# The output products of an attention block: 32 channels of o stacked under c2, the other 64 as half pieces

## The chip, the cores and the metric

The kernel runs on one core of a Trainium2 chip. The metric is the device time of one execution in microseconds: the median of 3 runs is 6416.27 us, the lowest 6413.48, the highest 6428.01. The profile is of one further execution.

## The reference

The input is x, four images of 96 channels and 128 x 128 pixels, all in f32. A state-space block (convolution, scans in four directions, normalisation over channels, a projection from 192 to 96 channels) comes first, and its result is normalised in groups. The second block takes that result, here called xnew, and computes:

```python
xr, x1, x2 = _relu_split_norm(x, sc1, sc2, res_coef, nc1, nc2)
y1 = NORM_SCALE * _layer_norm(_attn_conv(x1, x2, aw1, aw2, aw3))
y2 = NORM_SCALE * _layer_norm(_conv2d(x2, w_conv2, K // 2)) * x1
y = jnp.concatenate([y1, y2], axis=1)
return xr + _conv2d(y, w_full, 0) + b_full[None, :, None, None]
```

So for every pixel the output has a part that is linear in the value of xnew on each side of a threshold (the residual and xr), plus a matrix of 96 x 192 times the 192 values of y. 96 of those come from the attention convolution (o in the kernel) and 96 from an ordinary convolution (c2), normalised and multiplied by x1. The layer norms are over a whole image, so the last product can begin only when o and c2 of the image are complete and their means and variances known. The normalisation is folded into the weights and a bias.

## The kernel before

The images go one after the other. For an image b there is first a norm (`ssm_output`: the scan's result is normalised, projected and added to the input, giving xnew), a split (`split_norm`), the attention convolution (`attention`, products at L1477 and L1492, their results copied by ScalarE and combined by VectorE in `outputs`, L1550 to L1573) and last the close (`attn_output`), which makes the output of the image. Python generators emit the instructions: `co_run` emits the convolution of image b (the left side) and, between its steps, pieces of lighter work (the right side): norm and split of image b+1, then the close of image b-1. What remains of the right side is emitted before the next convolution begins. Each `yield` names an estimated cost in microseconds by which the two are dealt out.

For the first phase, up to the end of the scan, `in_order` (L339) ties every instruction to the one before it on its engine. After L2561 nothing does: the framework's planner orders the instructions of each engine by their place in the program and by when it expects them to be ready. The result is seen in the trace: the program emits the o product and the c2 product of one half, then of the other, and the trace has both halves' o products first and then both halves' c2 products. Each engine then runs its own list in order, and a wait holds what is behind it. Loads and stores go through SP's queue, also in order.

The close of images 0, 1 and 2 is `attn_output`, L2299 to L2341. The last image has its own form (`LastOutput`), which shares `own_weights`, `c2_weights`, `first_half` and `residual` with it. In `attn_output`:

- `own_weights` (L2259) forms mean and variance of o, scales the first 96 x 96 part of the weights by the inverse deviation into w1, and writes the bias as row 96 of w1 by two products of one row and a copy. `c2_weights` (L2224) does the same for c2, giving w2; its mean is in s2.
- The bias row is met by a row of ones: `with_ones` makes tiles of 97 partitions whose last row is set by GpSimd (L2278) once, and o is loaded into the first 96.
- An image is cut into NS = 16 tiles of SN = 1024 pixels, and each tile into two halves of CH = 512 pixels[...] (`part`, from the pool `psr`, which has two banks). Loads of the next tile are issued ahead: o (L2312), c2 and xx, which is xnew (L2315), 384 KB each, from DRAM.
- For a tile, ScalarE computes x1 (L2283), VectorE masks it (L2284), VectorE makes c2 = (c2 - mean) * x1 in place (L2326). `residual` makes e: ScalarE the upper line (L2288), VectorE the mask (L2289) and then e = xx * low + e (L2290).
- For each half, TensorE makes the product of w1 and o (97 rows, L2334) and, in the same bank, of w2 and c2 (96 rows, L2335). VectorE adds e and writes the result over x1 (L2337 for image 0; L2339 with another order of the pixels for images 1 and 2). A store takes x1 to the output (L2341).

The norm contains a projection of 192 channels to 96 (L1023 and L1028) in which 128 channels are one product and the other 64 lie as two pieces, each half of the pixels on one half of the partitions.

Of the kernel before, what the change touches and what calls it, by code (L numbers as in the profile page):

```python
# [9 lines left out]
F32 = mybir.dt.float32  # L10
BF16 = mybir.dt.bfloat16
AF = mybir.ActivationFunctionType
ALU = mybir.AluOpType
# [4 lines left out]
C = 96  # L18
H = W = 128
L = H * W  # L20
CH = 512
# [32 lines left out]
SN = 1024  # L54
# [17 lines left out]
def kernel(  # L72
# [26 lines left out]
    nc = tc.nc  # L99
# [6 lines left out]
    def load(src, name):  # L106
        t = const.tile(list(src.shape), F32, name=name, tag=name)
        nc.sync.dma_start(t, src)
        return t
# [44 lines left out]
    def filled(value, name, n=C, p=C):  # L154
        t = const.tile([p, n], F32, name=name, tag=name)
        nc.vector.memset(t, value)
        return t

    mean96 = filled(1.0 / C, "mean96")
# [17 lines left out]
    def col(name, width=1, bufs=None):  # L177
        return small.tile([C, width], F32, name=name, tag=name, bufs=bufs)

    def rsqrt(dst, var):  # L180

        t = col("rsq")
        nc.vector.tensor_scalar(t, var, GN_EPS, None, ALU.add)
        nc.scalar.activation(t, t, AF.Sqrt)
        nc.vector.reciprocal(dst, t)

    def combine(ps, stats, mat, name, mv=None):


        if mv is None:  # L190
            mv = small.tile([stats.shape[0], 2], F32, name="mv", tag=f"mv{stats.shape[0]}")
            nc.vector.bn_aggr(mv, stats)  # L192
        n = mv.shape[0]
        p1 = bank(ps)[:n, 0:2]
        nc.tensor.matmul(p1, lhsT=mat, rhs=mv, start=True, stop=True)  # L195
        r = small.tile([n, 2], F32, name=name, tag=name)
        nc.vector.tensor_copy(r, p1)
        d2 = small.tile([n, 1], F32, name=f"d2{n}", tag=f"d2{n}")
        nc.vector.tensor_sub(d2, mv[:, 0:1], r[:, 0:1])
        nc.vector.tensor_mul(d2, d2, d2)  # L200
        p2 = bank(ps)[:n, 0:2]
        nc.tensor.matmul(p2[:, 0:1], lhsT=mat, rhs=d2, start=True, stop=True)  # L202
        nc.vector.tensor_add(r[:, 1:2], r[:, 1:2], p2[:, 0:1])
        return r, mv
# [84 lines left out]
    def bank(ps):  # L289

        return ps.tile([128, CH], F32, name="bank", tag="bank")

    def part(ps, *shape):
        n = 1
        for d in shape[1:]:
            n *= d
        t = bank(ps)[: shape[0], :n]
        return t if len(shape) == 2 else t.rearrange("p (a b) -> p a b", b=shape[2])
# [1922 lines left out]
            yield from lift(H)  # L2221
            later.flush()

    def c2_weights(img, ps, pool):  # L2224


        n = NSTRIP
        mva, mvb = (pool.tile([128, 2], F32, name=f"mv_{i}") for i in "ab")
        for mv, st, p, e, k in (
            (mva, img.c2a, 96, 128, 4 * n - img.mapped),  # L2230
            (mvb, img.c2b, 0, 64, 2 * n - (not img.mapped)),
            (mvb, img.c2b, 64, 128, 2 * n - 1),
        ):
            v = st[p:e, :k].rearrange("p c s -> p (c s)")
            nc.vector.bn_aggr(mv[p:e], v)
        halves = ((mva[96:128], m96[96:128]), (mvb, mrows[img.mapped]))

        def over(n):
            pt = bank(ps)[:, 0:n]
            for i, (mv, mat) in enumerate(halves):  # L2240
                nc.tensor.matmul(
                    pt, lhsT=mat, rhs=mv[:, 0:n], start=(i == 0), stop=(i == 1)
                )
            return pt

        s2 = pool.tile([128, 2], F32, name="s2")
        nc.vector.tensor_copy(s2, over(2))
        for mv, p in ((mva, 96), (mvb, 0)):
            d = mv[p:128, 0:1]
            nc.vector.tensor_sub(d, d, s2[p:128, 0:1])  # L2250
            nc.vector.tensor_mul(d, d, d)
        nc.vector.tensor_add(s2[:, 1:2], s2[:, 1:2], over(1))
        r2 = col("r2")
        rsqrt(r2, s2[0:C, 1:2])
        w2 = pool.tile([C, C], F32, name="w2")
        nc.vector.tensor_scalar(w2, wful[:, 1], r2, None, ALU.mult)
        return s2, w2

    def own_weights(img, ps, pool):  # L2259

        so, _ = combine(ps, img.ost.rearrange("p c s -> p (c s)"), mean96, "so")
        ro = col("ro")
        rsqrt(ro, so[:, 1:2])
        w1 = pool.tile([128, C], F32, name="w1")
        nc.vector.tensor_scalar(w1[0:C], wful[:, 0], ro, None, ALU.mult)
        nso = col("nso")
        nc.vector.tensor_scalar(nso, so[:, 0:1], -1.0, None, ALU.mult)
        pt = bank(ps)[C : C + 1, 0:C]  # L2270
        nc.tensor.matmul(pt, lhsT=img.keep["low"][:, 1:2], rhs=ident, start=True, stop=False)
        nc.tensor.matmul(pt, lhsT=nso, rhs=w1[0:C], start=False, stop=True)  # L2272
        nc.vector.tensor_copy(w1[C : C + 1], pt)
        return w1[0 : C + 1]

    def with_ones(pool, name, bufs=None):
        y = pool.tile([128, SN], F32, name=name, tag=name, bufs=bufs)
        nc.gpsimd.memset(y[C : C + 1], 1.0)  # L2278
        return y[0 : C + 1]

    def first_half(img, xx, x1):
        thr, scale, shift = (img.keep[n] for n in ("thr", "scale", "shift"))
        nc.scalar.activation(x1, xx, AF.Identity, scale=scale[:, 0:1], bias=shift[:, 0:1])  # L2283
        nc.vector.scalar_tensor_tensor(x1, xx, thr, x1, ALU.is_gt, ALU.mult)  # L2284

    def residual(img, xx, e):
        up, low, thr = (img.keep[n] for n in ("up", "low", "thr"))
        nc.scalar.activation(e, xx, AF.Identity, scale=up[:, 0:1], bias=up[:, 1:2])  # L2288
        nc.vector.scalar_tensor_tensor(e, xx, thr, e, ALU.is_gt, ALU.mult)  # L2289
        nc.vector.scalar_tensor_tensor(e, xx, low[:, 0:1], e, ALU.mult, ALU.add)  # L2290

    def pixels(v):

        return v.rearrange("p (h j t) -> p h t j", j=TW, t=TN)

    def plain(v):
        return v.rearrange("p (h t j) -> p h t j", j=TW, t=TN)

    def attn_output(img, ps, side, share):  # L2299
        ob = out[img.b].rearrange("c h w -> c (h w)")  # L2300
        with (
            tc.tile_pool(name="f1", bufs=1, side=side) as p1,
            tc.tile_pool(name="f3", bufs=2, side=side) as p3,
        ):
            w1 = own_weights(img, ps, p1)
            s2, w2 = c2_weights(img, ps, p1)
            ones = [with_ones(p1, f"o{i}") for i in range(2)]

            def loads(t):
                o = ones[t % 2]  # L2310
                got = [o]
                nc.sync.dma_start(o[0:C], img.od[:, bass.ts(t, SN)])  # L2312
                for name, src in (("c2", img.c2d), ("xx", img.xnew)):
                    y = p3.tile([C, SN], F32, name=name)
                    nc.sync.dma_start(y, src[:, bass.ts(t, SN)])  # L2315
                    got.append(y)
                return got

            ahead = loads(0)
            for t in range(NS):  # L2320
                o, c2, xx = ahead
                if t + 1 < NS:
                    ahead = loads(t + 1)
                x1 = p3.tile([C, SN], F32, name="x1")
                first_half(img, xx, x1)
                nc.vector.scalar_tensor_tensor(  # L2326
                    c2, c2, s2[0:C, 0:1], x1, ALU.subtract, ALU.mult
                )
                e = p3.tile([C, SN], F32, name="e")
                residual(img, xx, e)  # L2330
                for h in range(2):
                    sl = bass.ts(h, CH)
                    pf = part(ps, C, CH)
                    nc.tensor.matmul(pf, lhsT=w1, rhs=o[:, sl], start=True, stop=False)  # L2334
                    nc.tensor.matmul(pf, lhsT=w2, rhs=c2[:, sl], start=False, stop=True)  # L2335
                    if img.mapped:
                        nc.vector.tensor_add(x1[:, sl], pf, e[:, sl])  # L2337
                    else:
                        nc.vector.tensor_add(plain(x1[:, sl]), pixels(pf), pixels(e[:, sl]))  # L2339
                    yield 2.6 * share  # L2340
                nc.sync.dma_start(ob[:, bass.ts(t, SN)], x1)  # L2341

# [103 lines left out]
    class Image:  # L2446
# [44 lines left out]
        def close(self, ps, side, share=1.0):  # L2491
            while not self.finished:
                at.later.tick()
            yield from attn_output(self, ps, side, share)
# [27 lines left out]
    with tc.tile_pool(name="wp", bufs=1, side="left") as wp:  # L2522
# [7 lines left out]
        for images, pace in (([0], 0.25), ([1], 0.75), ([2, 3], 1.35)):  # L2530
            left = projections(images, weights, stats, wp, psl)
            if images[0] == 0:
# [12 lines left out]
                got = next(others)  # L2545
                while not got:
                    next(left)
                    got = next(others)
# [25 lines left out]
    wful = load(w_full, "wful")  # L2574
# [123 lines left out]
```

## Time and profile before

| what | value |
|---|---|
| median of 3 runs | 6416.27 us |
| profiled execution | 6409.68 us, span 6407.8 us |
| mean granted clock of TensorE | 0.902 |
| busy share of the span | TensorE 82%, VectorE 73%, ScalarE 59%, GpSimd 51% |
| close of image 0: first o product, last evacuation starts | 4646.0 us, 4777.2 us |
| close of image 1 and 2: evacuations (L2339) start | 5461.2 to 5905.8 us |
| o products, L2334 | 192 instructions, 105.5 us busy |
| c2 products, L2335 | 192 instructions, 108.2 us busy |
| DMA | 1205.30 MB, 188 GB/s mean |

An f32 product of one half shows as two matmul instructions, so a tile has four of L2334 and four of L2335. Busy time counts overlapping instructions once, while the mean duration of one is counted in full; the durations of matmuls overlap, and what a product costs TensorE is seen from one start to the next. In a group, the idle time is that of the engine just ahead of the group's instructions, with what ended it.

### The profile page before, as it was taken

Reading aid. Unit: us, or ns where it says so; the run is one execution under the profiler, and the core shown is the slowest. Engines: PE = TensorE matmul, PEld = TensorE weight load, DVE = VectorE, ACT = ScalarE, POOL = GpSimd, SP = SyncE. Lnnn points to the kernel's source line nnn. Section 1 sums busy time; section 2 is a strip of 40 time slices with the busy share of each in tenths; the row PEclk is TensorE's granted clock in tenths of the full one; section 3 lists DMA queues with packets and bytes.
Section 4 is the critical chain, followed back from the end, with each engine's and each line's share of the span. In section 5 each row is a group of like instructions: output and inputs, shape, how many; then the busy total and the mean of one; then the engine's idle time right before and its main releaser. Section 6 shows DMA issues by size and latency. Waiting matters only on the chain. (4 is left out here: it accounts for less than half of the span.)

```text
span 6407.8 us, 76468 instructions
## 1 busy us (share of the span) xinstructions
PE 5253.4 (82%) x23264; PEld 2254.8 (35%) x23264; DVE 4699.9 (73%) x7132; ACT 3759.4 (59%) x4770; POOL 3238.6 (51%) x2476
## 2 busy tenths in 40 slices
PE   6889988987888643989988588977888877889888
PEld 2333322322222111444433234345333444345553
DVE  4247878988989768989844686468774687988767
ACT  1247767787787666777622465466644665545642
POOL 1326757978879554979822234436304365022310
PEclk9899989998999765999999799989989888999989
DMA  6766777775675766676667686665776656967668
GB/s 155 175 160 189 198 199 199 214 221 163 198 202 171 202 183 207 196 213 179 182 185 195 166 228 163 195 169 156 214 199 184 175 149 165 245 167 180 191 168 221
DMA packets 897706, 1205.30 MB, mean 188 GB/s; under 512 B 230644, under 2 KB 745642, under 8 KB 884816
## 3 DMA queue, kind: packets, MB, share of 16 engines
q1 hardware_dynamic: 866640, 1145.36, 65.5%
q0 software_dynamic: 16336, 38.51, 2.3%
q10 hardware_dynamic: 14320, 16.54, 0.9%
q8 instruction: 187, 3.06, 0.2%
q14 instruction: 223, 1.83, 0.1%
HBM read 777.82 MB, written 345.62 MB: 175 GB/s over the span
## 5 line engine op out<-in xcount | busy, mean ns | idle before, releaser
L633 PE MATMUL bank<-y,wp 128*128 128x512 f32 (+3 forms) x3584 | 1310.9, 622 | 83.8 <-DMA y<-y 41.0
L866 POOL TENSOR_TENSOR y<-y,dl 128x1024 f32<-128x1024 f32 x384 | 1058.5, 2757 | 263.0 <-DVE dl L858 240.3
L833 POOL TENSOR_TENSOR dl<-dl,u 128x1024 f32<-128x1024 f32 x384 | 1008.8, 2627 | 253.1 <-ACT dA L809 121.1
L854 DVE TENSOR_TENSOR_SCAN dA<-dA,pBC 128x512 f32<-128x512 f32 x768 | 981.6, 1278 | 30.7
L2169 PE MATMUL bank<-y,wn 128*64 128x384 f32 (+5 forms) x2408 | 680.1, 507 | 58.3 <-DMA y<-x1d 34.1
L1477 PE MATMUL two<-ya,wd 128*64 128x192 f32 (+3 forms) x2376 | 582.2, 414 | 174.0 <-ACT odd L1550 65.1
L633 PEld LDWEIGHTS bank<-y,wp 128*128 128x128 f32 (+3 forms) x3584 | 456.2, 168 | 749.3 <-issue 651.1
L858 DVE TENSOR_TENSOR dl<-dA,pBC 128x512 f32<-128x512 f32 x768 | 528.5, 688 | 255.8 <-PE pBC L747 183.8
L747 PE MATMUL pBC<-xr,wbc 60*128 60x512 bf16 (+1 forms) x1536 | 457.8, 404 | 311.5 <-DVE dA L854 239.1
L1938 ACT COPY yb<-ya 64x768 f32<-64x768 f32 (+1 forms) x660 | 537.7, 815 | 195.5 <-PE two L1477 113.8
L676 ACT ACTIVATE dl<-pd,dtb 128x512 f32<-128x512 f32 x768 | 485.5, 684 | 187.9 <-PE pd L747 171.5
L1477 PE MATMUL two<-yb,wd 128*64 128x192 f32 (+3 forms) x2376 | 559.0, 400 | 4.0 <-ACT yb L1938 4.0
L837 DVE TENSOR_TENSOR pBC<-dl,pBC 128x512 f32<-128x512 f32 x768 | 527.5, 687 | 8.8 <-POOL dl L833 7.8
L2169 PEld LDWEIGHTS bank<-y,wn 128*64 128x64 f32 (+3 forms) x2408 | 310.3, 169 | 357.2 <-issue 186.2
L809 ACT ACTIVATE dA<-dl,negA 128x1024 f32<-128x1024 f32 x384 | 420.3, 1141 | 2.3
L1477 PEld LDWEIGHTS two<-ya,wd 128*64 128x64 f32 (+1 forms) x2376 | 262.2, 165 | 370.9 <-ACT odd L1550 75.0
L676 ACT ACT_TABLE_LOAD x248 | 318.2, 1283 | 91.9 <-PE pd L747 79.7
L747 PEld LDWEIGHTS <-wbc 60*128 60x128 bf16 (+1 forms) x1536 | 103.1, 96 | 752.1 <-issue 739.3
L1477 PEld LDWEIGHTS two<-yb,wd 128*64 128x64 f32 (+1 forms) x2376 | 289.7, 167 | 150.5 <-issue 42.1
L1477 PE MATMUL two<-ya,wa 128*96 128x384 f32 (+1 forms) x528 | 231.2, 521 | 72.9 <-DMA ya<-vp 27.0
L1550 ACT COPY odd<-two 128x384 f32<-128x384 f32 (+5 forms) x176 | 115.8, 658 | 291.3 <-PE two L1492 179.1
L1406 POOL TENSOR_TENSOR pl<-x 96x256 f32<-96x256 f32 (+3 forms) x396 | 275.2, 710 | 0.0
(322 smaller groups left out, 9105.4 us busy)
## 6 DMA issues: line engine op xcount, KB each, us to landing
u<-zb SPq DMA_DIRECT2D x192, 1024.0 KB
yms<-y SPq DMA_DIRECT2D x96, 512.0 KB
xn<-xnew SPq DMA_DIRECT2D x128, 384.0 KB
ya<-vp SPq DMA_DIRECT2D x120, 336.0 KB
y<-y SPq DMA_DIRECT2D x128, 258.2 KB
zb<-z SPq DMA_DIRECT2D x64, 512.0 KB
y<-yms SPq DMA_DIRECT2D x64, 512.0 KB
ya<-x1p SPq DMA_DIRECT2D x90, 336.0 KB
```

The lines of the kernel that those rows point to most:

```text
L633: nc.tensor.matmul(blocks(pz[p:e]), lhsT=ws[k][:, d, c : c + e - p], rhs=window(ys[k], at, d, n), start=(i == 0), stop=(i == len(terms) - 1),)
L676: nc.scalar.activation(dst, src, AF.Softplus, bias=bias)
L747: nc.tensor.matmul(p, lhsT=w[rows], rhs=xr[rows, at : at + CH], start=True, stop=True)
L809: nc.scalar.activation(live[m]["dA"], live[m]["dl"], AF.Exp, scale=negA[:, g % 3, k : k + 1])
L833: nc.gpsimd.tensor_mul(t, t, u_view(n))
L837: nc.vector.tensor_mul(p, live[n]["dl"][:, bass.ts(half, CH)], p)
L854: nc.vector.tensor_tensor_scan(h, h, p, init, ALU.mult, ALU.add)
L858: nc.vector.tensor_mul(live[n]["dl"][:, sl], live[n]["dA"][:, sl], live[n]["C", half])
L866: nc.gpsimd.tensor_add(v, v, t.rearrange("p (a b) -> p a b", b=W))
L1477: nc.tensor.matmul(of(to[p:e], r), lhsT=w[:, i, c : c + e - p], rhs=tiles(t[k][PAIR[i]][:, SLOT[i]], o, r), start=(k == 0), stop=False,)
L1938: nc.scalar.copy(yb[k][64 * h - 64 : 64 * h, :, :n], ya[k][0:64, :, h * TN : h * TN + n])
L2169: nc.tensor.matmul(pc[p:e, :n].rearrange("p (h w) -> p h w", w=W), lhsT=w[:, c : c + e - p], rhs=v[:, :, 0:W], start=(i == 0), stop=(i == ...
```

## The change

Only `attn_output` and the helpers of its weights change. The product over 97 and 96 rows becomes a product over 128 rows and a half piece over 64:

- Channels 0 to 31 of o are loaded under the 96 channels of c2 into one tile of 128 partitions, and their weights lie under w2 in `stack[:, 0]`. One product per half then covers them.
- Channels 32 to 95 of o come as a tile of 128 partitions and 512 pixels: the first half of the pixels on partitions 0 to 63, the second half on 64 to 127. Their weights lie twice in `stack[:, 1]`, and each half's product takes 64 partitions. Both halves' results are in two banks that are taken together. A tile has five loads in place of three, of the same bytes.
- The weights w1 are moved to their places in the stack by three DMAs from GpSimd's queue for each image.
- There is no row of ones. The bias (the residual's constant plus the product of w1 and the negative mean of o) is a column `base`, and ScalarE makes low * xx + base in a third activation for each tile. That is written over x1 once the c2 operation has read it; VectorE then adds it to e in place of the former multiply and add. The last image's form still has the row of ones, through `own_weights`.
- All four products of a tile are emitted ahead of the two evacuations, in the order stacked, stacked, half piece, half piece.

```diff
-            w1 = own_weights(img, ps, p1)
-            s2, w2 = c2_weights(img, ps, p1)
-            ones = [with_ones(p1, f"o{i}") for i in range(2)]
+            ro, nso = own_scale(img, ps)
+            w1 = p1.tile([C, C], F32, name="w1")
+            nc.vector.tensor_scalar(w1, wful[:, 0], ro, None, ALU.mult)
+            pt = bank(ps)[:C, 0:1]
+            nc.tensor.matmul(pt, lhsT=w1, rhs=nso, start=True, stop=True)
+            base = col("base")
+            nc.vector.tensor_add(base, pt, img.keep["low"][:, 1:2])
+            stack = p1.tile([128, 2, C], F32, name="ws")
+            s2, _ = c2_weights(img, ps, p1, stack[0:C, 0])
+            nc.gpsimd.dma_start(stack[C:128, 0], w1[0:32])
+            for h in range(2):
+                nc.gpsimd.dma_start(stack[64 * h : 64 * h + 64, 1], w1[32:C])
 
             def loads(t):
-                o = ones[t % 2]
-                got = [o]
-                nc.sync.dma_start(o[0:C], img.od[:, bass.ts(t, SN)])
-                for name, src in (("c2", img.c2d), ("xx", img.xnew)):
-                    y = p3.tile([C, SN], F32, name=name)
-                    nc.sync.dma_start(y, src[:, bass.ts(t, SN)])
-                    got.append(y)
-                return got
+                c2 = p3.tile([128, SN], F32, name="c2")
+                o = p3.tile([128, CH], F32, name="o")
+                xx = p3.tile([C, SN], F32, name="xx")
+                nc.sync.dma_start(c2[0:C], img.c2d[:, bass.ts(t, SN)])
+                nc.sync.dma_start(c2[C:128], img.od[0:32, bass.ts(t, SN)])
+                nc.sync.dma_start(xx, img.xnew[:, bass.ts(t, SN)])
+                for h in range(2):
+                    nc.sync.dma_start(
+                        o[64 * h : 64 * h + 64], img.od[32:C, bass.ts(2 * t + h, CH)]
+                    )
+                return o, c2, xx
...
+                d = c2[0:C]
                 nc.vector.scalar_tensor_tensor(
-                    c2, c2, s2[0:C, 0:1], x1, ALU.subtract, ALU.mult
+                    d, d, s2[0:C, 0:1], x1, ALU.subtract, ALU.mult
                 )
                 e = p3.tile([C, SN], F32, name="e")
-                residual(img, xx, e)
+                nc.scalar.activation(e, xx, AF.Identity, scale=up[:, 0:1], bias=up[:, 1:2])
+                nc.scalar.activation(x1, xx, AF.Identity, scale=low[:, 0:1], bias=base)
+                nc.vector.scalar_tensor_tensor(e, xx, thr, e, ALU.is_gt, ALU.mult)
+                nc.vector.tensor_add(e, e, x1)
+                pf = [part(ps, C, CH) for _ in range(2)]
+                for h in range(2):
+                    nc.tensor.matmul(
+                        pf[h], lhsT=stack[:, 0], rhs=c2[:, bass.ts(h, CH)],
+                        start=True, stop=False,
+                    )
+                for h in range(2):
+                    p = slice(64 * h, 64 * h + 64)
+                    nc.tensor.matmul(
+                        pf[h], lhsT=stack[p, 1], rhs=o[p], start=False, stop=True
+                    )
                 for h in range(2):
                     sl = bass.ts(h, CH)
-                    pf = part(ps, C, CH)
-                    nc.tensor.matmul(pf, lhsT=w1, rhs=o[:, sl], start=True, stop=False)
-                    nc.tensor.matmul(pf, lhsT=w2, rhs=c2[:, sl], start=False, stop=True)
```

`own_scale` is the first part of the former `own_weights`, which now calls it; `c2_weights` takes a place for w2 from its caller.

More of the change, by code (lines that the diff above doesn't have):

```diff
@@ L2222, in direct_maps, with c2_weights @@
             later.flush()
-    def c2_weights(img, ps, pool):
+    def c2_weights(img, ps, pool, w2=None):
         n = NSTRIP
@@ L2254, in c2_weights, with own_scale @@
         rsqrt(r2, s2[0:C, 1:2])
-        w2 = pool.tile([C, C], F32, name="w2")
+        if w2 is None:
+            w2 = pool.tile([C, C], F32, name="w2")
         nc.vector.tensor_scalar(w2, wful[:, 1], r2, None, ALU.mult)
         return s2, w2
+    def own_scale(img, ps):
+        so, _ = combine(ps, img.ost.rearrange("p c s -> p (c s)"), mean96, "so")
+        ro, nso = col("ro"), col("nso")
+        rsqrt(ro, so[:, 1:2])
+        nc.vector.tensor_scalar(nso, so[:, 0:1], -1.0, None, ALU.mult)
+        return ro, nso
     def own_weights(img, ps, pool):
-        so, _ = combine(ps, img.ost.rearrange("p c s -> p (c s)"), mean96, "so")
-        ro = col("ro")
-        rsqrt(ro, so[:, 1:2])
+        ro, nso = own_scale(img, ps)
         w1 = pool.tile([128, C], F32, name="w1")
         nc.vector.tensor_scalar(w1[0:C], wful[:, 0], ro, None, ALU.mult)
-        nso = col("nso")
-        nc.vector.tensor_scalar(nso, so[:, 0:1], -1.0, None, ALU.mult)
         pt = bank(ps)[C : C + 1, 0:C]
@@ L2304, in attn_output @@
         ):
-            w1 = own_weights(img, ps, p1)
-            s2, w2 = c2_weights(img, ps, p1)
-            ones = [with_ones(p1, f"o{i}") for i in range(2)]
-            def loads(t):
-                o = ones[t % 2]
-                got = [o]
-                nc.sync.dma_start(o[0:C], img.od[:, bass.ts(t, SN)])
-                for name, src in (("c2", img.c2d), ("xx", img.xnew)):
-                    y = p3.tile([C, SN], F32, name=name)
-                    nc.sync.dma_start(y, src[:, bass.ts(t, SN)])
-                    got.append(y)
-                return got
+            ro, nso = own_scale(img, ps)
+            w1 = p1.tile([C, C], F32, name="w1")
[9 more added lines that the diff above has]
+                nc.gpsimd.dma_start(stack[64 * h : 64 * h + 64, 1], w1[32:C])
+            def loads(t):
+                c2 = p3.tile([128, SN], F32, name="c2")
[9 more added lines that the diff above has]
+                return o, c2, xx
             ahead = loads(0)
+            up, low, thr = (img.keep[n] for n in ("up", "low", "thr"))
             for t in range(NS):
@@ L2325, in attn_output @@
                 first_half(img, xx, x1)
+                d = c2[0:C]
                 nc.vector.scalar_tensor_tensor(
-                    c2, c2, s2[0:C, 0:1], x1, ALU.subtract, ALU.mult
+                    d, d, s2[0:C, 0:1], x1, ALU.subtract, ALU.mult
                 )
                 e = p3.tile([C, SN], F32, name="e")
-                residual(img, xx, e)
+                nc.scalar.activation(e, xx, AF.Identity, scale=up[:, 0:1], bias=up[:, 1:2])
[13 more added lines that the diff above has]
+                    )
                 for h in range(2):
                     sl = bass.ts(h, CH)
-                    pf = part(ps, C, CH)
-                    nc.tensor.matmul(pf, lhsT=w1, rhs=o[:, sl], start=True, stop=False)
-                    nc.tensor.matmul(pf, lhsT=w2, rhs=c2[:, sl], start=False, stop=True)
                     if img.mapped:
-                        nc.vector.tensor_add(x1[:, sl], pf, e[:, sl])
+                        nc.vector.tensor_add(x1[:, sl], pf[h], e[:, sl])
                     else:
-                        nc.vector.tensor_add(plain(x1[:, sl]), pixels(pf), pixels(e[:, sl]))
+                        nc.vector.tensor_add(plain(x1[:, sl]), pixels(pf[h]), pixels(e[:, sl]))
                     yield 2.6 * share
```

## The prediction

> **What bounds the kernel now.** I read the clock of the core (0.902 mean), then the page's engine totals, then windows cut to the three places where the changed lines run, then those lines' groups, then the order of TensorE's work, and last who waited.
>
> The page's first part gives the whole program, and the windows view gives the stretches of the three closes (images 0, 1 and 2), with busy time of each engine:
>
> ```profile
> PE 5253.4 (82%) x23264; PEld 2254.8 (35%) x23264; DVE 4699.9 (73%) x7132; ACT 3759.4 (59%) x4770; POOL 3238.6 (51%) x2476
> ...
> core 0: us, PE busy (x) PEld busy (x) DVE busy (x) ACT busy (x) POOL busy (x), PEclk, DMA share, GB/s
> 4640.00:4790.00 150.00, 122.17 (x366) 45.84 (x364) 121.13 (x145) 58.09 (x59) 14.66 (x15) 0.84 0.73 203
> 5445.00:5680.00 235.00, 208.14 (x726) 89.59 (x726) 203.49 (x278) 118.00 (x138) 8.79 (x15) 0.93 0.81 216
> 5680.00:5910.00 230.00, 209.98 (x1205) 112.85 (x1203) 190.25 (x264) 108.00 (x131) 68.85 (x84) 0.97 0.70 181
> ```
>
> The reader is to see two engines near the limit, not one. TensorE is busy 81, 89 and 91%; VectorE 81, 87 and 83%. ScalarE has room: 39, 50 and 47%. In the first close the two limits tie; in the third TensorE leads.
>
> The groups of the changed lines, from the view by lines (busy, mean ns, idle before):
>
> ```profile
> L2335 PE MATMUL bank<-c,w 96*96 96x512 f32 x192 | 108.2, 691 | 21.7 <-DVE c L2326 18.7 <-issue 2.7
> L2334 PE MATMUL bank<-o,w 97*96 97x512 f32 x192 | 105.5, 670 | 6.2 <-DVE x L2337 5.7 <-DVE x L2339 0.3
> L2290 DVE SCALAR_TENSOR_TENSOR e<-xx,kept,e 96x1024 f32<-96x1024 f32 x64 | 85.7, 1340 | 0.2
> L2288 ACT ACTIVATE e<-xx,kept 96x1024 f32<-96x1024 f32 x64 | 78.6, 1230 | 27.7 <-DMA xx<-xnew 19.1 <-DVE x L2337 6.5 <-DVE x L2284 2.1
> ```
>
> Each f32 product counts as two matmul instructions: 192 = 48 tiles x 2 halves x 2. Both products together keep TensorE busy 213.7 us, 4.45 us a tile. TensorE stands before the c2 product, because VectorE is late with c2 (L2326).
>
> Durations overlap, so I take the cost from starts. The timeline of TensorE, one tile of this close and one tile of the norm, whose projection (L1023, L1028) already has the form that the change brings:
>
> ```profile
> 5463.47 1.88 PE L2334 MATMUL bank<-o,w 97*96 97x512 f32 x4
> 5465.19 1.88 PE L2335 MATMUL bank<-c,w 96*96 96x512 f32 x4
> 5466.90 0.81 PE L1477 MATMUL two<-yb,wa 128*96 128x384 f32 x2
> ...
> 4995.53 1.88 PE L1023 MATMUL bank<-y,outws 128*96 128x512 f32 x4
> 4997.34 1.10 PE L1028 MATMUL bank<-yr,outws 64*96 64x512 f32 x4
> 4998.38 0.90 PE L1770 MATMUL two<-ident,ring 96*90 96x96 f32 x8
> ```
>
> From start to next start, the old pair takes 1.72 + 1.71 = 3.43 us; the stacked product and the half pieces take 1.81 + 1.04 = 2.85 us. The half pieces of the two halves run side by side.
>
> [...] four half pieces take 1.04 us where four full ones take 1.72, and the product ahead of them takes 1.81 instead of 1.72. [...] The nearest rows agree (683 ns at 512, L2337; 1221 ns at 1024, L2440). [...] the trace has 1.8 us median to landing, 0.54 us to issue, for the four that build the projection's stack.
>
> **The change part by part.**
>
> *TensorE's products.* 3.43 - 2.85 = 0.58 us a tile, x 48 = 27.8 us. A second way: the norm's window 4780 to 5030 holds 34.7 + 22.0 = 56.7 us busy for 16 tiles, 3.55 each, fragments included; the third close holds 29.8 + 32.6 = 62.4 us for 15 tiles, 4.16 each, at the same clock of 0.97. The difference, 0.61 us, agrees. So 9.3 us an image. How much reaches the end I must choose: where TensorE leads (third close, 91%) I take 0.95, in the second 0.75, in the first, where VectorE is level and already makes TensorE wait, 0.6. Sum: 9.3 x 2.3 = 21.4 us. Bounds: 0.3 a close (8 us) and all of it plus the 18.7 us wait on c2, if the planner fills it (46 us).
>
> *VectorE.* L2290 becomes a plain add of two SBUF tiles: 1.27 us undisturbed in the timeline becomes an estimated 1.22, so 48 x 0.05 = 2.4 us less; half passes: 1 us gained. The c2 operation and both evacuating adds stay.
>
> *ScalarE.* One more activation of 96x1024, 1.23 us (L2288), x 48 = 59 us, 21% on the 284 us that it is busy in the three windows. There is no table load at L2283 or L2288 and the function is the same. The room above hides the bulk, but the matmuls L1477 wait for ScalarE's copies: 8.8 us in the first close, 29.0 us in the other two. Half-proportional growth, 10%, is 3.8 us lost. If the cover fails, all of 59 us. This activation also brings a new wait: it overwrites x1, so it must follow the c2 operation on VectorE. Queued behind it on ScalarE are the copies yb (L1938) and ends and odd (L1550), for which TensorE waits. The planner can put them ahead of it; I count the wait into the 3.8, its bound is under rival C.
>
> *The bias.* The ones' memsets go (0.95 us, two an image, on GpSimd, which has 8.79 us of work in the second window): nothing. The bias row's two products and copy become one product and an add of 96x1: under 0.5 us an image either way.
>
> *The stack.* Three DMAs from GpSimd an image: 3 x 0.54 + 1.8 = 3.4 us after w1. Cover: w1 and w2 stand at 4608, 5430 and 5665 us; the first c2 products start at 4650.7, near 5460 and at 5676.8. At least 11 us of cover, so 0; I keep 1.5 us for the first tiles, where the o product can no longer go ahead of c2. If the cover is gone: GpSimd waits in order, once 207 us for a memset of the ring (5436 to 5644). w1 of image 1 came at 5429.7. Issues planned behind that wait would hold the whole close; the memset is later work, so I think it unlikely.
>
> *Loads.* Three a tile become five, same bytes: each tile issues two half pieces more, at 0.49 us (median of the norm's L953, the same form): 96 x 0.49 = 47 us of SP's queue time. Behind them stand the convolution's loads of ya and yc, and TensorE for those. SP waits for buffers far longer (124 us at L1921 alone between 4600 and 5920), so 0; with no cover 1 us a tile. 64 of o's 96 rows come as pieces of 2 KB in place of 4 KB, the form in which the norm loads yr; there TensorE and ScalarE stood 9.3 us on such loads over 64 tiles. I take 0, with 7 us (48 tiles) as the far end and no gain, the bytes being equal. The output's buffers are unchanged; o comes free later, with the half pieces instead of ahead of c2, which delays only the load two tiles on.
>
> *The planner* orders everything after the first phase anew. I cannot price that; some 10 us both ways goes into the range.
>
> Sum: -21.4 - 1.0 + 3.8 + 1.5 = -17 us. Against the profiled execution's 6409.7 us (span 6407.8 and 1.9 around it): 6392.6. The median of the runs is 6.6 us above that execution, so 6399 us.
>
> **The rivals.**
>
> *B, hidden.* VectorE is as full as TensorE, and TensorE waits for c2 anyway: in the old order the o product filled that wait; in the new it comes after c2. Then a third of the saving passes: -9.3 - 1 + 3.8 + 1.5 = -5 us, 6411. For it: 18.7 us of waits on L2326. Against: 91% in the third close.
>
> *C, slower by ScalarE.* The new activation waits in order for c2 with the convolution's copies behind it. Price: up to 1.27 us waiting and 1.23 us working a tile, 2.5 x 48 = 120 us of ScalarE; if a third reaches TensorE, 40 - 21 = +19 us, 6435. It decides from 0.45 us a tile reaching TensorE (21.4 / 48). For it: TensorE's waits end on ScalarE's copies more than on anything else in the last two closes. Against: ScalarE is idle half the time.
>
> *D, the halves do not meet.* At 4866 to 4870 us the planner set two half pieces, two full, two half, each 1.03 us: no saving, 4.1 us a tile against 3.43. All tiles so: +32 us of TensorE, three quarters passed, +5 for the rest: +29 us, 6445. For it: one tile of the norm did so. Against: most tiles show the 1.04 us, and the norm's mean of 3.55 has such tiles in it. A third of the tiles so: near -2 us.
>
> **How the numbers follow.** Faster as worked out, A: 0.46, own range 6383 to 6403. B: 0.26. C: 0.18. D: 0.10. The prediction is A's, 6399. The range is 6378 to 6434: below, A with all of the saving and a kind plan; above, C; D's full price is left out. 0.2% is 12.8 us, about what a measurement tells from no change. A is faster by that; B and the mild D are the same, 0.26; C and most of D are slower, 0.28.
>
> **What would show it.** Right: the new products' groups sum to some 170 to 185 us busy instead of 213.7; the half pieces start in fours 1.04 us apart; TensorE's share in the third close falls or that stretch shortens by some 8 us. B: L1477's stretches as long as before and more TensorE idle before the stacked product, on VectorE. C: waits of L1477 on ends, odd or yb well above 38 us, and ScalarE idle before the new activation on c2. D: half pieces in twos. Wrong altogether: a long wait of the first stacked product on GpSimd's DMAs, or differences far from the three closes, which the plan alone would make.

## The result and the profile after

The changed kernel takes 6476.01 us, median of 6 runs (6461.17 to 6483.95), against 6412.85 us of the kernel before on the same chips. The ratio is 1.0096, with a 95% interval of 1.0080 to 1.0111: slower by 1%, and 77 us from the predicted 6399. The profiled execution has a span of 6472.7 us at a mean granted clock of 0.895 (before 6407.8 at 0.902).

The page's first line of totals, and the windows view of the changed kernel at the stretches shown of the kernel before (columns as there):

```profile
PE 5253.2 (81%) x23258; PEld 2240.9 (35%) x23258; DVE 4695.3 (73%) x7132; ACT 3820.7 (59%) x4818; POOL 3213.4 (50%) x2479
```

```profile
4640.00:4790.00 150.00, 95.25 (x283) 30.02 (x282) 109.84 (x123) 70.74 (x67) 1.94 (x5) 0.77 0.69 186
5445.00:5680.00 235.00, 185.80 (x584) 70.23 (x584) 175.53 (x233) 125.08 (x139) 3.01 (x5) 0.89 0.78 206
5680.00:5910.00 230.00, 203.20 (x1183) 107.31 (x1182) 184.89 (x285) 120.22 (x142) 48.10 (x79) 0.93 0.66 172
```

The work in total is as before. In the second stretch TensorE does 584 instructions where it did 726, and VectorE 233 where it did 278. Over the whole program only ScalarE has become busier, by 61 us, nearly all of it the new activation (59.6 us). So it isn't an engine that has become the limit; all of them wait more.

The groups of the lines that answer to L2335, L2334, L2288 and L2290 of before (L2353 is the stacked product, L2359 the half pieces, L2348 the new activation, L2350 the add), from the view by lines:

```profile
L2353 PE MATMUL bank<-c,ws 128*96 128x512 f32 x192 | 128.8, 808 | 89.2 <-DVE c L2343 64.1 <-issue 24.0 <-DVE x L2365 1.1
L2359 PE MATMUL bank<-o,ws 64*96 64x512 f32 x192 | 65.8, 769 | 0.0
L2350 DVE TENSOR_TENSOR e<-e,x 96x1024 f32<-96x1024 f32 x48 | 59.7, 1244 | 40.1 <-ACT x L2348 39.8
L2348 ACT ACTIVATE x<-xx,base,kept 96x1024 f32<-96x1024 f32 x48 | 59.6, 1242 | 86.6 <-DVE c L2343 86.6
```

Products: 128.8 + 65.8 = 194.6 us, a saving of 19 and not the 27.8 expected; TensorE stands 89.2 us before them where it stood 21.7 + 6.2. One such stand, in the timeline of TensorE, is:

```profile
5595.84 0.89 PE L1477 MATMUL two<-ya,wa 128*96 128x384 f32 x2
5602.77 3.70 PE L2353 MATMUL bank<-c,ws 128*96 128x512 f32 x4 [6.05 <-issue]
5606.39 2.03 PE L2359 MATMUL bank<-o,ws 64*96 64x512 f32 x4
5608.35 1.15 PE L1477 MATMUL two<-yb,wa 128*96 128x384 f32 x2
```

and VectorE in the same stretch:

```profile
5596.91 0.53 DVE L1564 TENSOR_TENSOR wide<-odd,two 96x384 f32<-96x384 f32 x1
...
5598.53 0.56 DVE L1567 TENSOR_TENSOR two<-odd,two 96x384 f32<-96x384 f32 x1
5599.00 1.27 DVE L2287 SCALAR_TENSOR_TENSOR x<-xx,kept,x 96x1024 f32<-96x1024 f32 x1
5600.20 1.27 DVE L2349 SCALAR_TENSOR_TENSOR e<-xx,kept,e 96x1024 f32<-96x1024 f32 x1
5601.39 1.27 DVE L2343 SCALAR_TENSOR_TENSOR c<-c,s,x 96x1024 f32<-96x1024 f32 x1
```

The page calls the releaser "issue", but c2's operation (L2343) ends at 5602.66 and the product begins at 5602.77: TensorE waits for it. VectorE isn't idle then. Its list has the convolution's sums (L1564 to L1567), the mask and e's mask ahead of c2's operation, while TensorE's list has the tile's product ahead of the convolution's next ones (L1477 at 5608.35). In this stretch what stands behind the waiting product stays there: TensorE runs nothing from 5596.73 to 5602.77 us, and the convolution's next product starts behind the tile's own, 11.6 us after the end of the last one. The lists are the planner's, so the question is whether a list or one of the change's parts costs the 1%.

The second thing to see is 3.70 us for a stacked product that the prediction put at 1.81. This is taken up at the end.

### The profile page after: what moved, and what is told of

It reads as the page before. It is cut to its first block, busy times and chain, and to the rows that moved or that the text cites. A ratio compares the mean times of both kernels' runs of the same rounds, so it can differ in the third digit from the quotient of the medians.

```text
span 6472.7 us, 76565 instructions
## 1 busy us (share of the span) xinstructions
PE 5253.2 (81%) x23258; PEld 2240.9 (35%) x23258; DVE 4695.3 (73%) x7132; ACT 3820.7 (59%) x4818; POOL 3213.4 (50%) x2479
## 5 line engine op out<-in xcount | busy, mean ns | idle before, releaser
L1477 PE MATMUL two<-ya,wd 128*64 128x192 f32 (+3 forms) x2376 | 583.0, 417 | 176.5 <-ACT odd L1550 68.4
L1477 PE MATMUL two<-yb,wd 128*64 128x192 f32 (+3 forms) x2376 | 556.9, 402 | 10.3 <-ACT yb L1938 10.3
L1477 PEld LDWEIGHTS two<-ya,wd 128*64 128x64 f32 (+1 forms) x2376 | 258.7, 167 | 372.8 <-ACT odd L1550 79.1
L1477 PEld LDWEIGHTS two<-yb,wd 128*64 128x64 f32 (+1 forms) x2376 | 286.1, 168 | 155.4 <-issue 36.8
L1477 PE MATMUL two<-ya,wa 128*96 128x384 f32 (+1 forms) x528 | 229.2, 517 | 73.5 <-DMA wa<-watd 26.7
```

The source lines that it names most:

```text
L1477: nc.tensor.matmul(of(to[p:e], r), lhsT=w[:, i, c : c + e - p], rhs=tiles(t[k][PAIR[i]][:, SLOT[i]], o, r), start=(k == 0), stop=False,)
```

## The experiments

All ratios are to the kernel before on the same chip, with 95% intervals. Each kernel is planned anew, except where its lists are tied. They are told in the order in which they were run.

**The parts of the change.** The bias alone: products and loads of before, without the row of ones.

```diff
-            w1 = own_weights(img, ps, p1)
+            (base and w1 as in the change, products over 96 and 96 rows)
-                residual(img, xx, e)
+                nc.scalar.activation(e, xx, AF.Identity, scale=up[:, 0:1], bias=up[:, 1:2])
+                nc.scalar.activation(x1, xx, AF.Identity, scale=low[:, 0:1], bias=base)
```

> Only the bias part of the change: the products stay as before (o, then c2, for each half; o now 96 rows), the loads too, and ScalarE makes the line with the bias over x1. Cover theory (TensorE has nothing of a tile to do until c2 is made, since the stacked product comes first): no loss to speak of here, 6405 to 6425 us. Hand-over theory (ScalarE waits in order for VectorE's c2 and VectorE then for ScalarE): most of the 63 us is here, 6450 us or more.

Measured: 6423.11 us, 1.0021 (1.0012 to 1.0030). ScalarE waits 44.8 us for c2 here, and little of it arrives.

In the changed kernel, the third activation writes a tile of its own, so it needn't wait for c2:

```diff
-                nc.scalar.activation(x1, xx, AF.Identity, scale=low[:, 0:1], bias=base)
+                y = p1.tile([C, SN], F32, name="y1")
+                nc.scalar.activation(y, xx, AF.Identity, scale=low[:, 0:1], bias=base)
-                nc.vector.tensor_add(e, e, x1)
+                nc.vector.tensor_add(e, e, y)
```

> The changed kernel, but the line with the bias goes to a tile of its own, so that ScalarE need not wait for c2. Hand-over theory: ScalarE's 87 us of waits on c2 go, and most of the loss with them, 6425 us or less. Cover theory: the waits of TensorE on c2 stay, 6455 us or more.

Measured: 6461.90 us, 1.0075 (1.0052 to 1.0099). The 86.6 us of waits are gone, and about a fifth of the loss with them, which the intervals don't tell from nothing.

In the changed kernel, the half pieces ahead of the stacked products, so that TensorE has work while c2 is made:

```diff
-                    nc.tensor.matmul(pf[h], lhsT=stack[:, 0], rhs=c2[:, bass.ts(h, CH)], start=True, stop=False)
+                    nc.tensor.matmul(pf[h], lhsT=stack[p, 1], rhs=o[p], start=True, stop=False)
-                    nc.tensor.matmul(pf[h], lhsT=stack[p, 1], rhs=o[p], start=False, stop=True)
+                    nc.tensor.matmul(pf[h], lhsT=stack[:, 0], rhs=c2[:, bass.ts(h, CH)], start=False, stop=True)
```

> The changed kernel with the half pieces of o ahead of the stacked product, in the same banks. They need no c2, so TensorE can work while VectorE makes it. Cover theory: most of the loss goes, 6425 us or less, and TensorE's wait ahead of the stacked product falls from 64 us towards the 19 us of before. Hand-over theory: 6450 us or more.

Measured: 6475.39 us, 1.0103 (1.0083 to 1.0124). TensorE still stands 57.9 us before the stacked products. Then both of these edits together:

> The changed kernel with the half pieces first and the bias line in a tile of its own. Both theories: at or below the kernel before, 6390 to 6415 us, the saving of TensorE's time being kept. If it stays above 6440 us, neither is the cause, and the loads or the planner's order are left.

Measured: 6483.94 us, 1.0113 (1.0094 to 1.0133). The hand-over on ScalarE is gone here (its wait is 1.5 us) and the loss isn't, so it doesn't carry the loss. The wait of TensorE for c2 isn't gone: 86.4 us before the stacked products. So these two runs don't say what that wait costs; they say that work emitted ahead of it doesn't remove it, because c2 itself is late.

**Buffers.** Three buffers for c2, o and xx (`bufs=3`), so that loads find a free tile sooner; then this with the half pieces first.

> The changed kernel with three buffers in place of two for each of c2, o and xx; TensorE's order of instructions is the same as in the changed kernel, row by row. Loads theory (a tile's loads wait for the buffers that its forerunner's last products free, and on SP's queue also behind that tile's store, so the tiles run one after the other): the loads come a tile earlier and most of the loss goes, 6440 us or less. Order theory (the planner's new order of TensorE's work, with 12 tiles of the first close in a row and no convolution between): 6460 us or more.

> The half pieces first, and three buffers for each of c2, o and xx. Loads theory: TensorE can fill the wait for c2 and the loads are there, 6425 us or less. Order theory: as the run with the half pieces first alone, 6465 us or more.

Measured: 6471.97 us, 1.0088 (1.0058 to 1.0117), and 6473.12 us, 1.0093 (1.0066 to 1.0119). Buffers aren't it: TensorE stands 88.3 us before the stacked products with three buffers, as it did with two (89.2).

**The loads alone.** The kernel before, its products, bias and bytes untouched; only o comes in three pieces:

```diff
-                nc.sync.dma_start(o[0:C], img.od[:, bass.ts(t, SN)])
+                nc.sync.dma_start(o[0:32], img.od[0:32, bass.ts(t, SN)])
+                for h in range(2):
+                    nc.sync.dma_start(o[32:C, bass.ts(h, CH)], img.od[32:C, bass.ts(2 * t + h, CH)])
```

> The kernel before with o loaded in three pieces (32 channels whole, 64 channels in two halves of the pixels), so that a tile has five loads; the products stay. If the number of DMAs on SP's queue costs the time: 6440 us or more. If not: 6400 to 6425 us.

Measured: 6489.50 us, 1.0109 (1.0082 to 1.0137): the whole loss. Its windows view has the same second stretch, 611 instructions of TensorE for 726:

```profile
5445.00:5680.00 235.00, 194.00 (x611) 78.54 (x611) 180.72 (x233) 104.67 (x120) 0.12 (x1) 0.92 0.76 207
```

And the two products of the kernel before exchanged, c2's first, to price the lost cover alone:

```diff
-                    nc.tensor.matmul(pf, lhsT=w1, rhs=o[:, sl], start=True, stop=False)
-                    nc.tensor.matmul(pf, lhsT=w2, rhs=c2[:, sl], start=False, stop=True)
+                    nc.tensor.matmul(pf, lhsT=w2, rhs=c2[:, sl], start=True, stop=False)
+                    nc.tensor.matmul(pf, lhsT=w1, rhs=o[:, sl], start=False, stop=True)
```

> The kernel before with the two products of a half exchanged: c2 first, o second; all else stays. If having nothing for TensorE to do ahead of c2 is the cause (which the run with the half pieces first speaks against): 6440 us or more. If not: 6405 to 6430 us.

Measured: 6437.73 us, 1.0040 (1.0029 to 1.0051). That kernel is planned anew too, so this isn't purely the price of the cover.

**The same loads from another queue.** The changed kernel with the three loads of o's pieces issued by GpSimd, the same edit in five_loads, the changed kernel with only the store moved, and the changed kernel with one transfer for both half pieces:

```diff
-                nc.sync.dma_start(c2[C:128], img.od[0:32, bass.ts(t, SN)])
+                nc.gpsimd.dma_start(c2[C:128], img.od[0:32, bass.ts(t, SN)])
...
-                    nc.sync.dma_start(o[64 * h : 64 * h + 64], img.od[32:C, bass.ts(2 * t + h, CH)])
+                    nc.gpsimd.dma_start(o[64 * h : 64 * h + 64], img.od[32:C, bass.ts(2 * t + h, CH)])
```

> The changed kernel, with the three loads of o's pieces (32 rows under c2, two half pieces) issued by GpSimd; SP keeps c2, xx and the store. Theory Q (the loss is the five loads a tile in SP's one queue, behind the store, and the order that the planner makes of them): the loss of 1.0 to 1.1% goes; 6395 to 6425 us, ratio 0.997 to 1.002, the gap of 25 us between the closes of images 0 and 1 closes to under 10. Theory T (it is the transfers: more and smaller pieces, from whatever queue): 6455 to 6490. Theory W (the third activation's wait on c2 and the stacked product): 6455 or more, waits of that activation on c2 again near 87 us.

Measured: 6386.59 us, 0.9968 (0.9957 to 0.9979), faster than the kernel before. Its windows, and its groups of products and activation (the profile is of the slowest of its 20 executions, 6408.09 us):

```profile
4640.00:4790.00 150.00, 113.68 (x458) 45.91 (x456) 123.62 (x153) 83.75 (x85) 39.72 (x65) 0.86 0.81 229
5445.00:5680.00 235.00, 199.29 (x735) 80.62 (x735) 202.94 (x289) 141.21 (x160) 37.87 (x72) 0.96 0.86 231
```

```profile
L2353 PE MATMUL bank<-c,ws 128*96 128x512 f32 x192 | 108.2, 691 | 48.6 <-DVE c L2343 31.8 <-issue 12.0 <-DMA o<-od 2.3
...
L2348 ACT ACTIVATE x<-xx,base,kept 96x1024 f32<-96x1024 f32 x48 | 59.4, 1238 | 76.8 <-DVE c L2343 76.5
L2359 PE MATMUL bank<-o,ws 64*96 64x512 f32 x192 | 57.1, 674 | 0.0
```

735 instructions of TensorE in the second stretch for 584, and 108.2 + 57.1 = 165.3 us of products for 194.6. ScalarE still waits 76.8 us for c2, in a kernel that is faster than before: that wait costs nothing that can be seen.

> The kernel before, o loaded in three pieces by GpSimd, c2 and xx by SP: the same five loads a tile as in the run five_loads (1.0109), the same bytes and piece sizes, another queue. Theory Q: within 0.3% of the kernel before, 6395 to 6432. Theory T: 6460 to 6490, as five_loads.

Measured: 6400.22 us, 0.9988 (0.9971 to 1.0005): the five loads of 1.0109, from another queue. So the number and the size of the transfers don't cost 1% wherever they are issued; this kernel too has a plan of its own, and the runs further down take the two apart.

> The changed kernel with only the output's store issued by GpSimd; all five loads stay on SP, and no load stands behind a store that waits for VectorE's adds (118 us of waits in closes 1 and 2). If the loads are late because they stand behind the store (theory Q1), the time falls to 6400 to 6430. If what costs is that five loads a tile are in SP's queue at all, and displace the convolution's loads there or in the plan (theory Q2), 6450 to 6480.

Measured: 6437.73 us, 1.0040 (1.0026 to 1.0054), between both expectations: with the store away, over half of the loss is gone. Here too the plan is another, so that this run alone can't say by which way.

```diff
-                for h in range(2):
-                    nc.sync.dma_start(o[64 * h : 64 * h + 64], img.od[32:C, bass.ts(2 * t + h, CH)])
+                nc.sync.dma_start(o, img.od[32:C, bass.ts(t, SN)].rearrange("c (h n) -> h c n", h=2))
```

> The changed kernel with the two half pieces of o as one transfer on SP: four loads a tile. If each load more in SP's queue has its price (theories Q1, Q2), about half of the loss: 6430 to 6455. If the half pieces' rows of 2 KB cost (theory T), as the changed kernel, 6460 to 6485.

Measured: 6513.25 us, 1.0165 (1.0142 to 1.0188). A miss for every theory: fewer loads, more time.

**Queue and plan apart.** Moving loads to another queue also makes the planner order everything anew. To tell the two apart, each engine's list was tied, by ordering links that add no wait, to the list that the planner had made for another of these kernels:

```diff
+            for name in list_of_the_other_plan:
+                tc.add_manual_dep(late[name], last.name, NoSync, reason="order of a plan")
+                last = late[name]
```

SP's list is tied too. First, the five loads on SP in the plan of o_by_gpsimd:

> The changed kernel, its five loads on SP, with every engine's list tied to the order that the planner made for o_by_gpsimd (0.9968); o's loads stand in SP's list right behind c2's and xx's. Ties order only, they add no wait. Theory P (it is the planner's order that costs; SP's queue itself has room for five loads): 6385 to 6415. Theory S (SP's issuing, in order, of two loads more a tile costs by itself): 6450 or more. In between, both have a share.

Measured: 6399.13 us, 0.9985 (0.9971 to 0.9999). Second, the loads on GpSimd in the plan of the changed kernel (o's own loads, which that plan has in SP's list, go where the planner puts them in GpSimd's):

> The converse: o's pieces loaded by GpSimd, every engine's list tied to the order that the planner made for the changed kernel. Theory P: 6450 to 6480, as the changed kernel. Theory S: 6385 to 6420, as o_by_gpsimd.

Measured: 6477.65 us, 1.0113 (1.0084 to 1.0142). The second stretch in the windows view, first of sp_loads_other_plan and then of gpsimd_loads_changed_plan:

```profile
5445.00:5680.00 235.00, 199.85 (x735) 80.45 (x733) 202.78 (x288) 139.75 (x158) 10.58 (x20) 0.95 0.87 232
```

```profile
5445.00:5680.00 235.00, 186.27 (x586) 70.81 (x586) 174.00 (x231) 124.37 (x138) 29.97 (x64) 0.90 0.76 208
```

735 and 586, as 735 and 584 in the kernels whose lists they have, on whatever queue the loads stand, and in the traces TensorE, VectorE and ScalarE go through their work in the same order as there. The groups of sp_loads_other_plan (its lines are 27 further on: L2380 and L2386 are the products):

```profile
L2380 PE MATMUL bank<-c,ws 128*96 128x512 f32 x192 | 111.8, 712 | 52.0 <-DVE c L2370 35.2 <-issue 12.1 <-DVE x L2392 3.6
...
L2386 PE MATMUL bank<-o,ws 64*96 64x512 f32 x192 | 55.4, 655 | 0.0
```

| | plan of o_by_gpsimd | plan of the changed kernel |
|---|---|---|
| o's pieces from SP | 0.9985 (sp_loads_other_plan) | 1.0096 (the changed kernel) |
| o's pieces from GpSimd | 0.9968 (o_by_gpsimd) | 1.0113 (gpsimd_loads_changed_plan) |

Across, from one plan to the other, 1.1 to 1.45%; down, from one queue to the other, 0.17%, once up and once down, which the intervals don't tell from nothing. The order makes the loss, and the queue isn't needed for it. By order is meant that of all the lists together, SP's among them.

Then the price of the two loads alone, five_loads in the plan of the kernel before:

> The kernel before with o in three pieces on SP (five_loads, 1.0109), its lists tied to the planner's order of the kernel before, the two added loads right behind o's first. This prices two loads more a tile in SP's queue with nothing else moved. Theory P: 6400 to 6425. Theory S: 6460 to 6490. My prediction put it at 0, with 1 us a tile, 48 us, if nothing covers it (6455).

Measured: 6421.08 us, 1.0010 (0.9998 to 1.0022): +6 us by the ratio, interval -1 to +14. And the odd one, four_loads_on_sp in the plan that o_by_gpsimd has:

> four_loads_on_sp (one transfer for both half pieces, 1.0165, slower than with five loads, which the count of loads doesn't explain), with the lists tied to the plan of o_by_gpsimd. Theory P: 6385 to 6425. If the one transfer of both halves is itself slow on SP's queue: 6450 to 6515.

Measured: 6484.17 us, 1.0117 (1.0087 to 1.0147). The plan is not the main thing that ails this one. The waits on SP's queue, 5445 to 5910 us (line, what it waited for, total us, times, longest), show three large ones, two of them on the joint transfer; the last line is from sp_loads_other_plan:

```profile
SPq L2395 <- DVE x L2393: 26.9, 7, 11.5
SPq L2395 <- DMA o<-od: 22.0, 6, 6.1
SPq L1940 <- DMA o<-od: 18.3, 5, 5.6
...
SPq L1940 <- DMA o<-od: 0.6, 2, 0.4
```

Stores (L2395) and the convolution's loads (L1940) stand some 4 us at a time, 6.1 at most, and by this view start when the joint transfer has landed. Why this transfer holds the queue and the two halves don't is left open.

**The waits that are left.** o_by_gpsimd with the half pieces first, and with the activation's own tile as well (edits as above; both are planned anew, so their order isn't quite o_by_gpsimd's):

> o_by_gpsimd with each half's half piece ahead of its stacked product, so that TensorE has work while VectorE makes c2 (it waited 21.6 us for c2 in the closes of images 1 and 2, and ScalarE 59 us). If the wait on c2 were what is left, 10 to 20 us better: 6370 to 6380. If it is covered, the same as o_by_gpsimd within the planner's scatter: 6380 to 6400.

> The same, and the third activation writes a tile of its own, so that it doesn't wait for c2. If that wait of ScalarE costs anything, better than o_by_gpsimd_half_first by 5 to 15 us; if not, the same within 0.2%.

Measured: 6403.43 us, 0.9990 (0.9980 to 1.0000), and 6405.74 us, 0.9994 (0.9982 to 1.0006). Neither betters o_by_gpsimd, though the wait of the stacked product falls from 48.6 to 14.4 us in the first and that of the activation from 76.8 to 9.6 us in the second. In the first the half pieces now have 22.5 us of waits ahead of them, where they had none, and are busy for 78.9 us instead of 57.1, so this run doesn't show that a wait was free: it moved, and the products took longer. o_by_gpsimd has the lowest ratio of all kernels tried.

## Why the prediction was wrong

**The step that failed** is "The planner orders everything after the first phase anew. I cannot price that; some 10 us both ways goes into the range." Two orders of the same instructions lay 1.1 to 1.45% apart: 71 us (1.0096 against 0.9985, of 6412) with the loads on SP, 93 us with them on GpSimd. A range of 10 us for a term with no basis was a guess, and it took the place of the largest term in the sum. The part of the change that turned the plan was the one that was costed at 0, the loads: five_loads, with nothing else changed, got as bad a plan.

**Loads, "so 0".** Right for SP's queue itself: +6 us, -1 to +14, in an unchanged plan, against my far end of 7, and not the 48 that was the price with no cover. The step was right about the queue and blind to the loads' effect on the plan.

**TensorE's products.** Right, in an order that keeps TensorE busy. In sp_loads_other_plan the timeline has

```profile
5563.91 1.96 PE L2380 MATMUL bank<-c,ws 128*96 128x512 f32 x4 [1.41 <-DVE c L2370]
5565.80 1.10 PE L2386 MATMUL bank<-o,ws 64*96 64x512 f32 x4
5566.83 0.89 PE L1504 MATMUL two<-yb,wa 128*96 128x384 f32 x2
```

1.89 + 1.03 = 2.92 us from start to start; I had 2.85. Its groups sum to 111.8 + 55.4 = 167.2 us, and I asked for 170 to 185.

**VectorE's add.** The 1.22 us was my estimate, beside the 1221 ns of L2440 before; in the changed kernel the add (L2350) took 1244 ns in the mean.

**The sum of -17 us** is within what the change does in another order: -10 us in sp_loads_other_plan (interval -19 to -1), -21 us in o_by_gpsimd (-28 to -14), each by its ratio times the kernel before. That speaks for the terms of the change together, but doesn't show them: both figures hold the share of an order that isn't the one of before either, and how much of the agreement is luck is open. Singly, the 3.8 us for ScalarE and the shares of 0.6, 0.75 and 0.95 weren't tested.

**The bias, and rival C.** I foresaw the wait of the third activation on c2, and it came, 86.6 us. No run shows a cost of it: taking it away gave 1.0075 where the changed kernel has 1.0096, and 0.9994 against 0.9990 with o's loads on GpSimd, each time in a new plan; and o_by_gpsimd is faster than before with 76.8 us of it. C's own sign didn't come: TensorE's waits on ScalarE's copies in the first close and the last two are 4.8 + 22.4 us in the changed kernel (the latter from 5445 to 5970 us), against 8.8 + 29.0. (Of those 29.0 us the prediction put all to L1477; 4.7 are of L1645 and L1770.) C's number, 6435, and D's, 6445, would have been nearer the result than mine, with the wrong cause. B's wait on c2 came too: 64.1 us in the changed kernel, 35.2 in sp_loads_other_plan, 18.7 before. So the larger part of its growth is the order's, and 16.5 us remain in the other order. D fell: 48 of 48 tiles have their four half pieces side by side, a median of 1.10 us.

**What would show it.** "Differences far from the three closes, which the plan alone would make" was the wrong sign to look for. The plan's differences lie in the closes of images 1 and 2. From their first evacuation to their last, start to start, it is 444.6 us before (5461.2 to 5905.8), 487.2 in the changed kernel (5474.4 to 5961.6), 419.0 in sp_loads_other_plan and 484.3 in gpsimd_loads_changed_plan. Between the changed kernel and sp_loads_other_plan this is 68 us, where their spans differ by 63.4.

**What stays open:** why five loads in SP's queue lead the planner to this order; which engine's list in it, SP's included, does the harm; and how much of the small results of singly planned variants (1.0021, 1.0040, 0.9988, 0.9990) is their edit and how much their plan.

## What to carry to other kernels

Where a planner orders the work, an edit that no engine feels can still cost more than the edit that was meant, so a forecast should give the re-planning a range taken from how far plans of like kernels lie apart (here 1.1 to 1.45%), not from hope. To learn what an edit itself is worth, run it in the old order and in the new one; ties that order without waiting do that, and two plans by two variants make a table that settles it. Waits that stand out in the changed kernel (here 87 us on ScalarE) may be effects of the order: undo them before blaming them.

## What the runs showed of the hardware

In the changed kernel a wait of TensorE is seen twice: in the stand itself (6.05 us in the stretch shown above), and again in a lower clock after it (0.50 at the product behind, where 24 of the 48 had 1.00). The windows view of the changed kernel at that stand, and at the stacked product behind it (the granted clock of TensorE is the third number from the end), has

```profile
5596.00:5602.70 6.70, 0.72 (x2) 0.08 (x1) 6.60 (x9) 2.31 (x3) 0.00 (x0) 0.70 1.02 303
5602.77:5606.39 3.62, 3.62 (x4) 0.92 (x4) 1.22 (x1) 3.58 (x4) 0.00 (x0) 0.50 0.27 70
```

The clock falls within the stand (it was 1.00 from 5590 to 5596 us), and the product runs at 0.50. The changed kernel has 48 stacked products of four instructions. The 24 that ran at a granted clock of 1.00 throughout took 1.88 to 1.96 us, the 12 at 0.50 throughout took 3.70 to 3.73, and the other 12 lie between. In sp_loads_other_plan one ran at 0.50 throughout and 31 at 1.00.

Sorted by TensorE's idle time just ahead, in the changed kernel: under 0.5 us the median is 1.96 us; the six from 2.5 to 3.1 us took 2.60 to 3.70, and the 13 from 3.5 us on took 3.42 to 3.73, at a granted clock of 0.50 to 0.56. At 0.50 against 1.00 the product took 3.70 / 1.96 = 1.89 times as long. Behind the four stands of 2.56 us it took 2.60 to 3.28, at 0.57 to 0.72. The stand just ahead doesn't tell all: one product with 0.81 us ahead of it took 3.69. How long a stand it takes, and what lifts the clock again, is not shown.

Against sp_loads_other_plan the changed kernel has 63.4 us more of span. Its stands before the stacked products are 37.2 us longer (89.2 against 52.0), and its products are busy 27.4 us longer (194.6 against 167.2). The two together are of that size; that they are all of it is not shown.

The other fact is that a single transfer for both half pieces (1.0117 in the order of o_by_gpsimd) was slower than two transfers of the same bytes (0.9985), with the same order on TensorE, VectorE and ScalarE.
